# Sixteen batch ids in one register read instead of four

## The chip, the cores and the metric

The kernel runs on one core of a Trainium2 chip. The metric is the time of one execution on the device in microseconds (us); each kernel is run several times and the median is given. One execution is also profiled. The core has a matrix engine (PE, with the loading of its weights shown as PEld), a vector engine (DVE), a scalar engine (ACT), GpSimd (POOL) and SyncE (SP), which here issues the DMA transfers. Each engine runs its own list of instructions in order and waits on semaphores for the others. In the profile's rows an engine's name with a q (DVEq) is its instruction queue: register work and reads into registers, which are not counted as busy time of the engine.

## The reference

For each of 128 batches b, with an id `language_ids[b]` between 0 and 9 that selects the weights:

```python
w1 = W1[language_ids]
w2 = W2[language_ids]
h = jnp.einsum('bsh,bha->bsa', hidden_states, w1) + b1[language_ids][:, None, :]
h = jax.nn.relu(h)
adapted = jnp.einsum('bsa,bah->bsh', h, w2) + b2[language_ids][:, None, :]
x = hidden_states + adapted
...
return normed * gamma[language_ids][:, None, :] + beta[language_ids][:, None, :]
```

`normed` is `x` less its mean over the last axis, times `rsqrt(var + 1e-5)`, and the result is added to the input once more. x is (128, 128, 512) in float32; W1 is (10, 512, 128), W2 (10, 128, 512).

## The kernel before

One batch is one tile of 128 rows by 512. For each batch PE turns x by four transposes (`pxT`, line 440), ACT copies that to SBUF (`xT`, 444), PE multiplies by W1 (`down`, 463: four products, eight matmuls in the trace), ACT applies the bias and relu (`relu`, 471), PE multiplies by W2 (`up`, 477 or 485, into one of five PSUM tiles `py`), DVE adds the residual and its sum (`residual`, 503), ACT sums the squares (526), DVE scales by gamma (`scale`, 569) and finishes with rstd and the addend (`finish`, 578). POOL prepares two addends, x + b2 (450) and x + beta (457). SP loads x in pairs of batches and stores the outputs in pairs. For the first 17 batches SP fetches W1 of the batch's id from HBM (`load_first`, 276); later W1 of all ids lies in SBUF, and ACT or POOL copies the batch's part (`stage_w1`, 431), apart from some batches that SP loads (403, 692).

W2, b2, gamma and beta of all ten ids lie side by side in SBUF, and an instruction picks the batch's part by an address in a register of its own engine. So each of the five engines needs each id that it uses in its registers. The ids are loaded once into SBUF and clamped (`lang`, a row of 128 integers on one partition, line 253). `lid(b, engine)` (line 255) gives the register of batch b on an engine. When it is first asked for a batch of a group of four, it emits one instruction, `TENSOR_LOAD` (line 258), which reads the four ids of the group from `lang` into four registers; the other three batches of the group get theirs from the same read.

The order of the instructions is written out: the steps of all batches are put in a list `plan` with a due time counted in batches (`b` plus an offset from the table `STEPS`), sorted and emitted; the opening and the last batches are a plain list of calls. `keep` ties each instruction behind the one before on its engine. The reads have due times of their own: at `b + 0.99` ACT and PE ask for batch b + 5 and POOL for b + 6, so a read is emitted there when that batch begins a group. DVE's stand right behind `scale(b)` for each b that is a multiple of four, and read the group of b + 4. SP's come before the load that needs them.

Of the kernel before, what the change touches and what calls it, by code (L numbers as in the profile page):

```python
# [13 lines left out]
ET = mybir.EngineType  # L14
PSUM = bass.MemoryType.PSUM

P = 128
G = 4
X = 2
EPS = 1e-5  # L20
FIRST = 17
# [122 lines left out]
def cond_resid_kernel(ctx: ExitStack, tc: tile.TileContext, x, itok, W1, b1, W2, b2, gamma, beta, out):  # L144
# [11 lines left out]
    KC = H // P  # L156
    NG = B // G
    assert S == P and A == P and B % G == 0 and H % P == 0

# [3 lines left out]
    def keep(ins):  # L163

        engine = ins.ins.engine
        if engine in last:
            tc.add_manual_dep(ins.ins, last[engine], behind, reason="kept order")
        last[engine] = ins.ins.name
        return ins
# [16 lines left out]
    def load_x(g):  # L186
        t = xp.tile([P, X, H], FP, tag="x", name=f"x_{g}")
        keep(nc.sync.dma_start(out=t, in_=x[g * X : (g + 1) * X].rearrange("b s h -> s b h")))
        xs[g] = t

    def xb(b):
        return xs[b // X][:, b % X, :]

# [7 lines left out]
    def load_part(lo, hi, engine=nc.sync):  # L201
        xs[lo // X] = xp.tile([P, X, H], FP, tag="x", name=f"x_{lo // X}")
        keep(engine.dma_start(out=xs[lo // X], in_=x[lo:hi].rearrange("b s h -> s b h")))

# [41 lines left out]
    lids, w1s = {}, {}  # L246
# [4 lines left out]
    lang = const.tile([1, B], I32, name="lang")  # L251
# [1 line left out]
    keep(nc.vector.tensor_scalar(lang, lang, 0, L - 1, ALU.max, ALU.min))  # L253

    def lid(b, engine):
        g = b // G
        if (g, engine) not in lids:
            loads, vals = nc.values_load_multi_w_load_instructions(  # L258
                lang[0:1, g * G : (g + 1) * G],
                engines=[engine],  # L260
                min_val=0,
                max_val=L - 1,
                skip_runtime_bounds_check_because="clamped on the chip to 0..L-1 above",
            )
            for ins in loads:
                keep(ins)
            lids[g, engine] = vals
        return lids[g, engine][b % G]

# [1 line left out]
    def load_first(b):  # L273
        w1s[b] = wp.tile([P, KC, A], FP, tag="w1s", name=f"w1s_{b}")
        src = W1[bass.ds(lid(b, ET.SP), 1)].rearrange("o (p k) a -> p (o k a)", k=KC)
        keep(nc.sync.dma_start(out=w1s[b].rearrange("p k a -> p (k a)"), in_=src))  # L276
# [59 lines left out]
    def spread(r, copier):  # L336
        t = (beta_b, gamma_b, b2_b)[r // L]
        row = p_y.tile([P, H], FP, tag="y", name=f"row_{r}")
        pick_r = pick[:, r : r + 1].to_broadcast([96, P])
        keep(nc.tensor.matmul(row, lhsT=pick_r, rhs=parts[:96, :], start=True, stop=True))  # L340
        dst = t[:, r % L * H : (r % L + 1) * H]
        if copier is nc.scalar:
            keep(nc.scalar.copy(dst, row))  # L343
        else:
            keep(nc.vector.tensor_copy(dst, row))
# [9 lines left out]
    def shuffle_rows(lo, hi):  # L355
        for r in range(lo, hi):
            t = (beta_b, gamma_b, b2_b)[r // L]
            keep(nc.vector.stream_shuffle(t[:, r % L * H : (r % L + 1) * H], fours[0], [r] * 32))  # L358
# [8 lines left out]
    def of(parts, b):  # L367
        if b < len(parts[0]):
            return parts[0][b]
        return parts[1][b % steady] if b < closing else parts[2][b - closing]  # L370
# [16 lines left out]
    def b2_by_vector(b):  # L387
        return kind(b) == "D"
# [10 lines left out]
    def load_rows(b):  # L399
        w1s[b] = wp.tile([P, KC, A], FP, tag="w1s", name=f"w1s_{b}")  # L400
        rows = W1[bass.ds(lid(b, ET.SP), 1)].rearrange("o (i k r) a -> i (o r) k a", i=4, k=KC)
        for i in range(4):
            keep(nc.sync.dma_start(out=w1s[b][32 * i : 32 * (i + 1)], in_=rows[i]))
# [21 lines left out]
    def stage_w1(b):  # L425
        w1s[b] = wp.tile([P, KC, A], FP, tag="w1s", name=f"w1s_{b}")
        gpsimd = turn(b) == "c"
        v = lid(b, ET.Pool if gpsimd else ET.Activation)
        src = w1.rearrange("p l k a -> p (l k a)")[:, bass.ds(v * (KC * A), KC * A)]
        dst = w1s[b].rearrange("p k a -> p (k a)")  # L430
        keep(nc.gpsimd.tensor_copy(dst, src) if gpsimd else nc.scalar.copy(dst, src))  # L431
# [152 lines left out]
    def on(b):  # L584
        return 0 <= b < B
# [133 lines left out]
    x_turn(0)  # L719
    transpose_b1()  # L720
    spread(11, nc.scalar)
    for n in (0, G):
        lid(n, ET.PE)
    shuffle_rows(0, 10)
    x_turn(1)
    spread(12, nc.scalar)
# [31 lines left out]
    def at(when, step, *args):  # L758
        plan.append((when, len(plan), step, args))

    def when(name, b):
        return b + of(STEPS[name], b)

    for b in range(B):
        if b >= 20 and b % X == 0:
            at(b + X_STEPS[b // X - 10], load_x, b // X)
# [29 lines left out]
    def at_pair(g, key, step, *args):  # L796
        if g < E // 2 - 3 or (step, *args) in begun:
            at(key, step, *args)

    for g in range(E // 2 - 1):  # L800
        b = 2 * g
        for n in (b, b + 1):
            if b2_by_vector(n):
                at_pair(g, when("vb2", n), vector_b2, n)
            at_pair(g, when("stat", n), residual, n)
            at_pair(g, when("square", n), square, n)
        at_pair(g, when("means", b), scalar_means, g)
        at_pair(g, when("root", b), deviation, g)
        for n in (1, 2, 3):
            at_pair(g, when(f"n{n}", b), rstd, g, n)  # L810
        for n in (b, b + 1):
            at_pair(g, when("scale", n), scale, n)
            at_pair(g, when("end", n), finish, n)
        if b % G == 0 and on(b + G):
            at_pair(g, when("scale", b) + 0.001, lid, b + G, ET.DVE)
        at_pair(g, when("store", b), store, g)

    for _, _, step, args in sorted(plan, key=lambda step: step[:2]):
# [190 lines left out]
```

## Time and profile before

| | us |
|---|---|
| median of 3 runs | 300.58 |
| lowest and highest run | 299.26, 300.98 |
| the profiled execution | 300.62 |
| its span, first to last instruction | 298.9 |

TensorE's granted clock was 0.997 on average. The rows of the profile read: line, engine, operation, tile written <- tiles read, shape, count. In a timeline the first column is the start in us from the span's start, the second the duration of the group, and a bracket at the end gives the idle time of the engine before it and what ended it. The view of one line lists the number of its instructions and their shortest, median and longest duration in ns, with the first and last start.

### The profile page before, as it was taken

What the parts mean: (1) busy time and instruction counts of PE and PEld (TensorE: products, weight loads), DVE (VectorE), ACT (ScalarE), POOL (GpSimd) and SP (SyncE); (2) the same over time, 40 slices, a digit from 0 to 9 for tenths busy, and PEclk for the clock granted to TensorE, in tenths of its full rate; (3) what the DMA queues carried; (4) which work ended last, traced back from release to release, by engine and by line L of the source; (5) the groups of instructions that cost most, each with busy time, mean ns of one, the idle gap of its engine ahead of it and who ended that gap; (6) DMA issues with size and microseconds to landing.
All of it is one profiled execution on the core that took longest, in us unless ns stands there. A gap on an engine that the chain in (4) does not pass through costs nothing.

```text
span 298.9 us, 7366 instructions
## 1 busy us (share of the span) xinstructions
PE 290.5 (97%) x1783; PEld 215.7 (72%) x1783; DVE 288.5 (97%) x775; ACT 274.4 (92%) x761; POOL 276.8 (93%) x239
## 2 busy tenths in 40 slices
PE   7899999999999999999999999999999999999993
PEld 3658777777776777767777777777777777777760
DVE  6989999999999999899999999999999999999996
ACT  5878789999999999989999999999999999899993
POOL 1299998999999999999899999999899999999992
PEclk9999999999999999999999999999999999999998
DMA  6999999955978798986999399986989879884907
GB/s 226 392 388 368 345 330 401 404 221 182 325 242 315 232 315 208 374 278 211 326 303 356 134 302 289 335 276 217 333 220 397 288 258 281 314 274 147 313 4 281
DMA packets 61100, 85.22 MB, mean 285 GB/s; under 512 B 4057, under 2 KB 25060, under 8 KB 61058
## 3 DMA queue, kind: packets, MB, share of 16 engines
q1 hardware_dynamic: 60998, 84.71, 84.1%
q8 instruction: 15, 0.25, 0.3%
q14 instruction: 27, 0.22, 0.2%
q10 hardware_dynamic: 60, 0.05, 0.1%
HBM read 51.19 MB, written 33.55 MB: 284 GB/s over the span
## 4 chain that ended last, share of the span: by engine, by line
PE 75%; DMA 9%; POOL 6%; DVE 3%; issue 3%; SPq 1%; POOLq 1%; ACT 1%; ACTq 0%; DVEq 0%
PE ph L463 30%; PE py L485 23%; PE pxT L440 14%; PE py L477 8%; POOL o L457 3%; DMA out_dram<-o 3%; DMA w<-in_L_cond_W_dram 3%; POOL r L450 2%; DMA x<-in_x_dram 2%; DVE py L503 1%; DVE o L663 1%; SPq L276 1%; POOLq L258 1%; DVE n L669 0%; DVE py L569 0%
## 5 line engine op out<-in xcount | busy, mean ns | idle before, releaser
L457 POOL TENSOR_TENSOR o<-x,beta_b 128x512 f32<-128x512 f32 x121 | 153.8, 1297 | 14.4 <-DVE beta_b L358 11.6
L463 PEld LDWEIGHTS ph<-xT,w1s 128*128 128x128 f32 x1024 | 126.8, 192 | 14.8 <-ACT hT L471 8.5
L463 PE MATMUL ph<-xT,w1s 128*128 128x128 f32 x1024 | 135.5, 275 | 0.3 <-DMA w1s<-in_L_cond_W_dram 0.2
L450 POOL TENSOR_TENSOR r<-x,b_b 128x512 f32<-128x512 f32 x83 | 107.1, 1299 | 1.6 <-DMA x<-in_x_dram 1.6
L485 PE MATMUL py<-w,hT 128*128 x196 | 101.1, 598 | 0.2 <-DMA w<-in_L_cond_W_dram 0.2
L440 PEld LDWEIGHTS pxT<-ident,x 128*128 128x128 f32 x468 | 59.9, 150 | 53.4 <-issue 39.9
L569 DVE SCALAR_TENSOR_TENSOR py<-py,nmean,gamma_b 128x512 f32<-128x512 f32 x124 | 93.1, 752 | 0.0
L578 DVE SCALAR_TENSOR_TENSOR o<-py,rstd,o 128x512 f32<-128x512 f32 x116 | 85.7, 746 | 2.7 <-DVE py L569 1.6
L526 ACT ACTIVATE sq<-py,sum 128x512 f32<-128x512 f32 x124 | 85.5, 690 | 0.4 <-DVE rstd L545 0.3
L444 ACT COPY xT<-pxT 128x512 f32<-128x512 f32 x117 | 68.6, 586 | 5.6 <-PE pxT L440 5.5
L440 PE MATMUL pxT<-ident,x 128*128 128x128 f32 x468 | 71.2, 275 | 1.3 <-ACT gamma_b L343 0.7
L503 DVE SCALAR_TENSOR_TENSOR py<-py,r 128x512 f32<-128x512 f32 x88 | 60.8, 691 | 0.7 <-PE py L485 0.5
L471 ACT ACTIVATE hT<-ph,b1T 128x128 f32<-128x128 f32 x128 | 47.3, 369 | 8.2 <-PE ph L463 5.9
L431 ACT COPY w1s<-w 128x512 f32 x80 | 48.6, 618 | 1.2 <-issue 1.2
L485 PEld LDWEIGHTS py<-w,hT 128*128 128x128 f32 x196 | 29.9, 192 | 2.4 <-DMA w<-in_L_cond_W_dram 0.7
L477 PE MATMUL py<-w,hT 128*128 x60 | 30.7, 594 | 0.0
L526 ACT ACTIVATION_READ_ACCUMULATOR sq<-py,sum 128x1 f32 x124 | 25.5, 205 | 0.0
L503 DVE SCALAR_TENSOR_TENSOR py<-py,b_b 128x512 f32<-128x512 f32 x30 | 20.6, 688 | 0.0
L423 ACT COPY py<-x 128x512 f32<-128x512 f32 x30 | 17.9, 598 | 0.2 <-DVE o L578 0.2
L536 ACT ACTIVATE root<-ssq,eps 128x2 f32<-128x2 f32 x62 | 16.8, 271 | 0.4
L517 ACT ACTIVATE nmean<-sum 128x2 f32<-128x2 f32 x61 | 12.6, 207 | 0.5 <-DVE py L503 0.2
L503 DVE DVE_READ_ACCUMULATOR py<-py,r 128x1 f32 x88 | 12.3, 140 | 0.0
(80 smaller groups left out, 149.4 us busy)
## 6 DMA issues: line engine op xcount, KB each, us to landing
x<-in_x_dram SPq DMA_DIRECT2D x64, 512.0 KB, 5.6
out_dram<-o SPq DMA_DIRECT2D x62, 512.0 KB, 4.5
w1s<-in_L_cond_W_dram SPq DMA_DIRECT2D x25, 256.0 KB, 7.4
w1s<-in_L_cond_W_dram SPq DMA_DIRECT2D x44, 64.0 KB, 4.9
x<-in_x_dram SPq DMA_DIRECT2D x44, 64.0 KB, 2.3
w<-in_L_cond_W_dram SPq DMA_DIRECT2D x4, 640.0 KB, 8.1
w<-in_L_cond_W_dram SPq DMA_DIRECT2D x1, 1792.0 KB, 9.8
w<-in_L_cond_W_dram SPq DMA_DIRECT2D x1, 768.0 KB, 5.3
```

What stands on the lines that cost most here:

```text
L431: keep(nc.gpsimd.tensor_copy(dst, src) if gpsimd else nc.scalar.copy(dst, src))
L440: keep(nc.tensor.transpose(pxs[b][:, k, :], cols, ident))
L444: keep(nc.scalar.copy(xT[b], pxs.pop(b)))
L450: keep(nc.gpsimd.tensor_tensor(rs[b], xb(b), b2_b[:, bass.ds(v * H, H)], ALU.add))
L457: keep(nc.gpsimd.tensor_tensor(os[g][:, j, :], xb(b), beta_b[:, bass.ds(v * H, H)], ALU.add))
L463: nc.tensor.matmul(phs[b], lhsT=w1s[b][:, k, :], rhs=xT_of(b, k), start=(k == 0), stop=(k == KC - 1))
L477: keep(nc.tensor.matmul(ys[b], lhsT=hT[b], rhs=cols, start=False, stop=True, skip_group_check=True))
L485: keep(nc.tensor.matmul(ys[b], lhsT=hT[b], rhs=w2[:, bass.ds(v * H, H)], start=not m, stop=True))
L503: nc.vector.scalar_tensor_tensor(ys[b], ys[b], 1.0, r, ALU.mult, ALU.add, accum_out=sum_of(b))
L526: nc.scalar.activation(sq, ys[b], AF.Square, bias=col(sums, b), scale=-float(H), accum_out=col(ssqs, b))
L569: nc.vector.scalar_tensor_tensor(ys[b], ys[b], col(nmeans, b), gamma_b[:, bass.ds(v * H, H)], ALU.add, ALU.mult)
L578: nc.vector.scalar_tensor_tensor(o, ys[b], rstds[g][:, j : j + 1], o, ALU.mult, ALU.add)
```

## The change

A group is now sixteen batches for `lid`: one read brings sixteen ids into sixteen registers. `G = 4` remains for other uses. In the opening PE's two reads become one. In the pair loop DVE's read stands behind `scale(b)` for b a multiple of 16 and reads the group of b + 16. The reads of ACT, PE, POOL and SP follow from `lid` itself.

```diff
+IDS = 16
...
     def lid(b, engine):
-        g = b // G
+        g = b // IDS
         if (g, engine) not in lids:
             loads, vals = nc.values_load_multi_w_load_instructions(
-                lang[0:1, g * G : (g + 1) * G],
+                lang[0:1, g * IDS : (g + 1) * IDS],
...
-        return lids[g, engine][b % G]
+        return lids[g, engine][b % IDS]
...
-    for n in (0, G):
-        lid(n, ET.PE)
+    lid(0, ET.PE)
...
-        if b % G == 0 and on(b + G):
-            at_pair(g, when("scale", b) + 0.001, lid, b + G, ET.DVE)
+        if b % IDS == 0 and on(b + IDS):
+            at_pair(g, when("scale", b) + 0.001, lid, b + IDS, ET.DVE)
```

The lists of PE, DVE, ACT and POOL have 32 reads each before and 8 each with the change; SP's has 22 and then 8. No other instruction is added, removed or moved on any engine. Two places show it (all line numbers of the changed kernel are one higher).

DVE behind `scale(44)`, about 119 us into the span; `py` is the tile of a batch in PSUM, `o` the output. Before:

```order
L503 SCALAR_TENSOR_TENSOR py_2389,sum_2391<-py_2389,r_2308 128x512
L545 SCALAR_TENSOR_TENSOR rstd_2424<-part_2385,root_2384 128x2
L569 ISA
L569 SCALAR_TENSOR_TENSOR py_2226<-py_2226,nmean_2369,gamma_b 128x512
L258 TENSOR_LOAD lang
L578 SCALAR_TENSOR_TENSOR o_2194<-py_2288,rstd_2424,o_2194 128x512
```

With the change:

```order
L504 SCALAR_TENSOR_TENSOR py_2482,sum_2484<-py_2482,r_2419 128x512
L546 SCALAR_TENSOR_TENSOR rstd_2517<-part_2478,root_2477 128x2
L570 ISA
L570 SCALAR_TENSOR_TENSOR py_2331<-py_2331,nmean_2462,gamma_b 128x512
L579 SCALAR_TENSOR_TENSOR o_2299<-py_2399,rstd_2517,o_2299 128x512
```

The read of batches 48 to 51 is gone from this place; those ids come with the read behind `scale(32)`, where one stood before too, as DVE's list has it now:

```order
L570 ISA
L570 SCALAR_TENSOR_TENSOR py_1795<-py_1795,nmean_1891,gamma_b 128x512
L259 TENSOR_LOAD lang
L504 SCALAR_TENSOR_TENSOR py_1879,sum_1952<-py_1879,r_1863 128x512
L541 SCALAR_TENSOR_TENSOR part_1907<-ssq_1876,root_1906 128x2
```

That read is about 91 us into the span before; it keeps its place, and reads sixteen ids where it read four.

## Prediction

> **What bounds the kernel now.** I read the page first: busy shares, then the chain of waits.
>
> ```profile
> PE 290.5 (97%) x1783; PEld 215.7 (72%) x1783; DVE 288.5 (97%) x775; ACT 274.4 (92%) x761; POOL 276.8 (93%) x239
> PE 75%; DMA 9%; POOL 6%; DVE 3%; issue 3%; SPq 1%; POOLq 1%; ACT 1%; ACTq 0%; DVEq 0%
> ```
>
> PE is the bound, with DVE as busy as PE. A change can only gain what PE still loses between its matmuls, and DVE and ACT have little slack to take a delay. So the questions are what the reads of the ids (line 258) cost their engines, and how much of that reaches PE. The view of that line, all of the execution:
>
> ```profile
> L258 PEldq TENSOR_LOAD <-lang x32: 328/333/1140, 5.2 to 268.6; - x32
> L258 ACTq TENSOR_LOAD <-lang x32: 304/310/948, 8.0 to 268.6; - x32
> L258 DVEq TENSOR_LOAD <-lang x32: 340/344/1834, 18.5 to 273.7; - x32
> ```
>
> The columns are minimum/median/maximum in ns. A read of four ids is 0.31 to 0.34 us, whatever the engine, but some are far longer. Does one hold its engine up? The timeline of DVE around its two longest:
>
> ```profile
> L258 DVEq TENSOR_LOAD <-lang x1: 1834/1834/1834, 119.1 to 119.1; - x1
> 121.08 1.41 DVE L578 SCALAR_TENSOR_TENSOR o<-py,rstd,o 128x512 f32<-128x512 f32 x2 [0.84 <-DVE py L569]
> L258 DVEq TENSOR_LOAD <-lang x1: 1496/1496/1496, 223.2 to 223.2; - x1
> 224.80 1.41 DVE L578 SCALAR_TENSOR_TENSOR o<-py,rstd,o 128x512 f32<-128x512 f32 x2 [0.43 <-DVE py L569]
> ```
>
> L578 follows the read in the program, and both times it starts 0.1 to 0.2 us after the read has ended (119.1 + 1.83 = 120.9; 223.2 + 1.50 = 224.7). The bracket names L569, the instruction that ended last, yet what is waited for is the read. Thus a read is taken up ahead of the engine's own work and hides under it as long as it is shorter than its **room**, the time from its start to the start of the next instruction; beyond that the engine idles. ACT shows the same, and here the chain names the read:
>
> ```profile
> 132.57 0.52 ACTq L258
> 133.62 0.62 ACT L431 COPY w1s<-w 128x512 f32 x1 [0.53 <-issue]
> 168.04 0.62 ACT L431 COPY w1s<-w 128x512 f32 x1 [0.46 <-issue]
> ```
>
> **What the reads that go away cost PE.** The timeline of PE over these places:
>
> ```profile
> 125.96 0.60 PE L440 MATMUL pxT<-ident,x 128*128 128x128 f32 x4
> 126.56 1.12 PE L485 MATMUL py<-w,hT 128*128 x2
> 127.52 1.05 PE L463 MATMUL ph<-xT,w1s 128*128 128x128 f32 x8
> 128.55 1.13 PE L485 MATMUL py<-w,hT 128*128 x2
> ...
> 133.90 0.60 PE L440 MATMUL pxT<-ident,x 128*128 128x128 f32 x4
> 134.56 1.16 PE L463 MATMUL ph<-xT,w1s 128*128 128x128 f32 x8
> 135.55 1.02 PE L485 MATMUL py<-w,hT 128*128 x2
> ...
> 168.39 0.60 PE L440 MATMUL pxT<-ident,x 128*128 128x128 f32 x4
> 168.98 1.16 PE L463 MATMUL ph<-xT,w1s 128*128 128x128 f32 x8
> 169.97 1.02 PE L485 MATMUL py<-w,hT 128*128 x2
> ...
> 230.29 1.11 PE L485 MATMUL py<-w,hT 128*128 x2
> 231.24 1.05 PE L463 MATMUL ph<-xT,w1s 128*128 128x128 f32 x8
> 232.27 1.12 PE L485 MATMUL py<-w,hT 128*128 x2
> 233.23 0.60 PE L440 MATMUL pxT<-ident,x 128*128 128x128 f32 x4
> ```
>
> Undisturbed, a group starts 0.44 us after four pxT, 0.89 after eight ph, 0.86 after two py (rows 105.79 to 107.98 of the next fence). Here it is 0.60, 0.96, 1.03 after the long DVE read (0.40 too much), 0.66 and 0.99 after the ACT read of 132 (0.32), 0.59 and 0.99 after that of 167 (0.25), and 0.95, 1.03, 0.96 after the DVE read of 223 (0.33). Sum 1.30 us of PE for 0.84 + 0.53 + 0.46 + 0.43 = 2.26 us of idle engine, so **0.58 us of PE per us lost on DVE or ACT**.
>
> All four reads go: with sixteen ids the reads that stay are those where a batch of DVE's pair loop, or the batch that ACT and PE look ahead to, is a multiple of 16, and these four stand at others. Gain: **-1.3 us**. The other reads that go were hidden and give nothing.
>
> **What the reads that stay cost.** Eight stay on each engine, with 16 ids each. No row shows such a read. Bounds: 0.33 us, if it is one trip whatever it brings, and 4 x 0.33 = 1.32, if each id is a trip. The engines' minima (304, 328, 340) are too close together to tell. I take trips: a sequencer instruction without a read is short,
>
> ```profile
> L569 DVEq FUSED_REGOPS  x124: 57/57/57, 20.5 to 292.5; - x124
> ```
>
> so of DVE's 344 ns some 287 belong to four ids, 72 ns each, and sixteen make 57 + 16 x 72 = **1.2 us**, nearer to the high end. Now the rooms. PE, at one of the kept places:
>
> ```profile
> L258 PEldq TENSOR_LOAD <-lang x1: 331/331/331, 105.7 to 105.7; - x1
> 105.79 1.05 PE L463 MATMUL ph<-xT,w1s 128*128 128x128 f32 x8
> 106.68 0.60 PE L440 MATMUL pxT<-ident,x 128*128 128x128 f32 x4
> 107.12 1.02 PE L477 MATMUL py<-w,hT 128*128 x2
> 107.98 0.72 PE L463 MATMUL ph<-xT,w1s 128*128 128x128 f32 x5
> ```
>
> L477 is next after the read: room 1.42 us. A read of 1.2 and 0.1 to 0.3 to get going again nearly fills it: 0 to 0.14 lost at each of seven places, I take 0.07: **+0.5**. DVE, two kept places:
>
> ```profile
> L258 DVEq TENSOR_LOAD <-lang x1: 341/341/341, 90.7 to 90.7; - x1
> 91.44 0.69 DVE L503 SCALAR_TENSOR_TENSOR py<-py,r 128x512 f32<-128x512 f32 x1
> L258 DVEq TENSOR_LOAD <-lang x1: 346/346/346, 21.1 to 21.1; - x1
> 21.80 0.15 DVE L540 SCALAR_TENSOR_TENSOR part<-ssq,root 128x2 f32<-128x2 f32 x1
> ```
>
> Rooms 0.74 and 0.7, where 1.3 is wanted: 0.6 lost at each, 0.1 to 0.2 at two more (estimated), and some 0.4 at the first read, which only just precedes its user: 1.8 us. ACT has a room of 0.9 at a kept place, and there the read is long besides:
>
> ```profile
> L258 ACTq TENSOR_LOAD <-lang x1: 621/621/621, 244.6 to 244.6; - x1
> 245.49 0.37 ACT L471 ACTIVATE hT<-ph,b1T 128x128 f32<-128x128 f32 x1
> ```
>
> With one more such place and 0.1 here and there I put ACT at 1.2 us in all (an estimate). At 0.58, 3.0 us are **+1.7**. Long reads: kept places had them too, 621 ns on ACT above, and on PE and DVE
>
> ```profile
> L258 PEldq TENSOR_LOAD <-lang x1: 1060/1060/1060, 244.1 to 244.1; - x1
> L258 DVEq TENSOR_LOAD <-lang x1: 962/962/962, 56.3 to 56.3; - x1
> ```
>
> If their excess (0.73, 0.31, 0.62) comes once per read as now, PE loses about 0.6 and the others 0.93 x 0.58 = 0.5: **+1.1**. If it comes per id it is four times that, about +4.4.
>
> Taken at nothing: SP's first read holds back the first W1 loads by 0.9 us, with x and a part of W2 issued ahead of them for the DMA engines to work on; without that cover it costs 0.9. POOL's reads lie under its additions, some of them ahead. PE's two first reads become one, under the load of W2 that the first up waits for. Register work stays as it is.
>
> Sum: -1.3 + 0.5 + 1.7 + 1.1 = **+2.0 us** on the profiled execution's 300.62 (span 298.9 and 1.7 around it; the median of the runs is 300.58): **302.6 us**. Its own range: 301.0 (long reads and PE's share at nothing) to 304.3 (DVE and ACT losing twice the 3.0 us).
>
> [...]
>
> **The rivals.**
>
> *One trip whatever the count*: a read stays near 0.33 us and fits every room. Then only the gain is left, with some 0.3 (an estimate) for shorter delays behind other long reads that I did not count: 300.62 - 1.3 - 0.3 = **299.0**, faster. For it: four ids in 0.34, no more than six register instructions of 57 ns. Against it: nothing but the argument above. [...]
>
> *Trips, but covered*: a read takes 1.0 to 1.1, PE's rooms hold it, DVE and ACT make up their 2 to 3 us before it reaches PE's buffers (five py). Half of the +1.7 and nothing else: 300.62 - 1.3 + 0.9 = **300.2**, no change. For it: the read of 962 ns at 56.3 left no idle on DVE.
>
> *Long reads grow with the ids*: one of 1.06 becomes 4.2 and PE stands still for almost 3 us: 302.6 - 1.1 + 4.4 = **305.9**. It decides once an id's trip, not the read, meets the traffic. For it: every engine's maximum is three to five times its median, so what lengthens a read is no engine's own. Against it: no row tells whether a long read lost its time once or on each id.
>
> *Slow trips*: with sixteen, every trip is as slow as in the read of 962 ns, 0.24 us, so 3.9 a read; PE loses 3.9 + 0.1 - 1.42 = 2.6 at seven places, 18 us: 300.62 - 1.3 + 18 = **317**. Against it: 0.33 for four nearly always. [...]
>
> **How the numbers follow.** Chances: forecast 0.45, one trip 0.27, covered 0.15, growing 0.09, slow 0.04. About 0.5% (1.5 us) is what a measurement of this kernel can tell from no change. Slower: 0.40 of the forecast's, 0.01 of covered, 0.13 of the last two, together 0.54. Same: 0.05, 0.07 of one trip, 0.10 of covered: 0.22. Faster: 0.20 of one trip, 0.04 of covered: 0.24. The range 298.7 to 306.3 takes in all but the slow trip and some of the ends.
>
> **What would show it.** Line 258's row: 8 reads an engine, a minimum of 1.1 to 1.4 us is right, 0.35 is the first rival. The idle of 0.84, 0.53, 0.46 and 0.43 is gone. New idle after the read stands on DVE near 22 and 91 and on ACT near 245; py on PE after the kept reads is on time or 0.1 late. If the reads are 1.2 us and the time is still below 300.6, my factor of 0.58 is wrong; if PE waits for over 1 us at several reads, long ones grow.

## The result, and the profile after

| | before | the change |
|---|---|---|
| median | 300.7 | 304.87 |
| lowest and highest of 4 runs each | 299.26, 300.98 | 303.96, 305.48 |
| ratio to before, 95% interval | | 1.0146 [1.0104, 1.0187] |
| the profiled execution | 300.62 | 303.96 |
| its span | 298.9 | 302.2 |

The change makes the kernel slower by 1.5%, 4.2 us, where 2.0 were forecast. First the view of the line of the reads in the changed kernel, with shortest, median and longest duration in ns:

```profile
L259 SPq TENSOR_LOAD <-lang x8: 979/1028/3042, 3.1 to 245.6; - x8
L259 POOLq TENSOR_LOAD <-lang x8: 1049/1060/1894, 3.1 to 236.0; - x8
L259 PEldq TENSOR_LOAD <-lang x8: 1110/1122/1780, 5.2 to 247.1; - x8
L259 ACTq TENSOR_LOAD <-lang x8: 1009/1022/1222, 8.0 to 247.7; - x8
L259 DVEq TENSOR_LOAD <-lang x8: 1095/1210/2297, 20.7 to 232.3; - x8
```

There are eight reads an engine, and the shortest is 3.2 to 3.4 times as long as with four ids, not four times. Against the minima of before, twelve more ids cost PE 1110 - 328 = 782 ns and DVE 1095 - 340 = 755, 63 to 65 ns each; some 67 to 88 ns are left that do not depend on the count. The median is close to the minimum on four engines. On DVE it is not: several of its reads are long, and the longest takes twice the minimum. The timeline of DVE around three of them, each read with the instruction that follows it:

```profile
L259 DVEq TENSOR_LOAD <-lang x1: 1352/1352/1352, 20.7 to 20.7; - x1
22.33 0.70 DVE L496 TENSOR_TENSOR py<-py,b_b 128x512 f32<-128x512 f32 x1 [0.96 <-ACT sq L527]
L259 DVEq TENSOR_LOAD <-lang x1: 2297/2297/2297, 127.3 to 127.3; - x1
129.76 0.70 DVE L504 SCALAR_TENSOR_TENSOR py<-py,r 128x512 f32<-128x512 f32 x1 [1.41 <-PE py L486]
L259 DVEq TENSOR_LOAD <-lang x1: 1669/1669/1669, 162.8 to 162.8; - x1
164.66 0.70 DVE L504 SCALAR_TENSOR_TENSOR py<-py,r 128x512 f32<-128x512 f32 x1 [0.60 <-POOL o L458]
```

127.3 + 2.30 is 129.6, and DVE goes on at 129.76 after 1.41 us of idle time; 162.8 + 1.67 is 164.5, and it goes on at 164.66. The brackets name PE and POOL, but the read ends last, as it did behind the long reads of before. Of the 0.96 us in the opening only some 0.4 are new: the same instruction waited for PE there before,

```profile
19.79 0.70 DVE L495 TENSOR_TENSOR py<-py,b_b 128x512 f32<-128x512 f32 x1 [0.56 <-PE py L485]
```

which is counted with the other idle time of before in the table below. A fourth read, of 1.31 us at 232.3, leaves 0.46. A read of the shortest kind leaves nothing where its room is large enough:

```profile
L259 DVEq TENSOR_LOAD <-lang x1: 1095/1095/1095, 58.4 to 58.4; - x1
L259 DVEq TENSOR_LOAD <-lang x1: 1098/1098/1098, 92.6 to 92.6; - x1
```

PE, in the opening and behind its longest read, which starts at 247.1:

```profile
11.44 1.10 PE L441 MATMUL pxT<-ident,x 128*128 128x128 f32 x4 [1.91 <-DMA x<-in_x_dram]
12.76 1.82 PE L464 MATMUL ph<-xT,w1s 128*128 128x128 f32 x8
...
249.13 1.12 PE L478 MATMUL py<-w,hT 128*128 x2 [0.41 <-issue]
```

The 1780 ns read costs PE 0.41 us as the bracket has it; the seven others show nothing of the kind. The opening is new. PE waits 1.91 us for a pair of x, and the eight matmuls of the next `ph` take 1.82 us where 1.05 is usual. The windows view of PE (length, busy time, instructions, granted clock, DMA share, GB/s) says why, with before's row below:

```profile
10.90:14.30 3.40, 2.86 (x13) 0.51 1.03 392
```

```profile
10.90:14.30 3.40, 3.40 (x27) 1.00 1.05 394
```

The granted clock was 0.51 for 3.4 us. The first matmul of W2 (`up`, line 486) then starts at 18.40 in place of 16.16.

To see how much of this counts I split DVE's idle time, in every profile taken, into the gaps of over 0.1 us in which a read ends, at most 0.4 us before DVE goes on (called **read idle** from here on), and all the others between DVE's first and last instruction:

| kernel | read idle | other idle | span |
|---|---|---|---|
| before | 1.57 | 5.24 | 298.9 |
| the change | 3.44 | 6.51 | 302.2 |
| the change again (last experiment but one) | 5.41 | 5.01 | 302.9 |

DVE's own work is the same in all (288.5, 288.7 and 288.8 us). In the first profile of the change 1.9 us of the 3.3 are more read idle, and 1.3 are more of the other kind, in a late opening; in the second 3.8 of the 4.0 are read idle and the opening isn't late. Some 0.5 of the 1.9 and of the 3.8 is the wait for PE that counted as other idle before.

### The profile page after: what moved, and what is told of

It reads as the page before. It is cut to its first block, busy times and chain, and to the rows that moved or that the text cites. A ratio compares the mean times of both kernels' runs of the same rounds, so it can differ in the third digit from the quotient of the medians.

```text
span 302.2 us, 7266 instructions
## 1 busy us (share of the span) xinstructions
PE 291.5 (96%) x1783; PEld 216.8 (72%) x1783; DVE 288.7 (96%) x775; ACT 274.6 (91%) x761; POOL 276.9 (92%) x239
```

## The experiments

What had to be told apart: does the loss come from DVE's reads (that they hold DVE where they are), from SP's first read (which holds back the first loads), or from what PE, ACT and POOL pay? All kernels below make the number of ids a choice for each engine; each adds to this only what its own diff shows:

```diff
-IDS = 16
+IDS = {ET.SP: 4, ET.PE: 16, ET.Activation: 16, ET.DVE: 16, ET.Pool: 16}
...
-        g = b // IDS
+        n = IDS[engine]
+        g = b // n * n
...
-                lang[0:1, g * IDS : (g + 1) * IDS],
+                lang[0:1, g : g + n],
...
-        return lids[g, engine][b % IDS]
+        return lids[g, engine][b - g]
...
-        if b % IDS == 0 and on(b + IDS):
-            at_pair(g, when("scale", b) + 0.001, lid, b + IDS, ET.DVE)
+        n = IDS[ET.DVE]
+        if b % n == 0 and on(b + n):
+            at_pair(g, when("scale", b) + 0.001, lid, b + n, ET.DVE)
```

The line of the reads is 260 in them. Ratios are to before on the same chip, five rounds each, with the 95% interval in brackets.

**SP back to four ids, the rest sixteen.** This is the diff above as it stands.

> Sixteen ids on PE, DVE, ACT and POOL, four on SP. Theory A (the opening: SP's first read of sixteen ids, 1.18 us instead of 0.50, sends the first loads out 0.7 us later, and the x of batches 2 and 3 lands too late for PE's transposes): PE's wait for that x (1.91 us at 11.4 in the changed kernel) is gone, py starts at 16.2 us again and not at 18.4, the span falls by about 2.2 us from 302.2 to 300, the time to 302.6, ratio to before 1.004 to 1.009. Theory B (the delays behind the long reads on DVE, ACT and PE later on make up most of the loss): the span stays above 301.5 and the ratio at 1.012 or more.

1.0068 [1.0043, 1.0094], median 302.88: about half of the loss is gone. PE's wait for x in the opening is gone too. DVE's reads at the same places are still long: 1.11 us of idle time behind the one near 57, 1.03 near 126, 0.83 near 161. So SP has a part, and DVE another.

**SP alone with sixteen.**

```diff
+IDS = {ET.SP: 16, ET.PE: 4, ET.Activation: 4, ET.DVE: 4, ET.Pool: 4}
```

> Sixteen ids on SP alone, four on the others. Theory A: the opening loses its 2.2 us here too (py from 18.4 us on, PE waits near 11.4 for x), nothing else changes; time 302.4 to 303.2, ratio 1.006 to 1.010. Theory B: SP's reads lie ahead of the transfers by enough, time as before, ratio 0.998 to 1.003.

1.0011 [0.999, 1.0032]. The theory that put some 2 us on SP's first read falls at this size. Its opening is as late as the change's, in the timeline and the windows of PE:

```profile
11.24 1.10 PE L442 MATMUL pxT<-ident,x 128*128 128x128 f32 x4 [1.70 <-DMA x<-in_x_dram]
10.90:14.30 3.40, 3.06 (x14) 0.54 1.03 395
```

Its `up` starts at 18.41, 2.25 us behind before, and PE ends its work 1.15 behind: half of a late opening was won back here. In the median of twelve runs little of it is seen.

**DVE's reads in another place, all sixteen.** The read of the next sixteen batches stands behind `scale(4)`, `scale(20)` and so on, in place of `scale(0)`, `scale(16)`; nothing else differs from the change.

```diff
+IDS = {ET.SP: 16, ET.PE: 16, ET.Activation: 16, ET.DVE: 16, ET.Pool: 16}
...
+        if b % n == 4 and on(b - 4 + n):
+            at_pair(g, when("scale", b) + 0.001, lid, b - 4 + n, ET.DVE)
```

> The changed kernel, with DVE's reads four batches later: behind scale(b) for b = 4, 20, 36, ... instead of 0, 16, 32, ...; still sixteen ids, the same group. In the kernel before the reads of four ids at these places were 341 to 345 ns each time from b = 36 on, with rooms of 0.98 to 1.67 us. Theory C (a place decides, by its room and by whether reads there are lengthened): the reads are 1.10 us there, DVE's idle of 1.41, 0.60 and 0.46 us behind them falls to 0.2 us or less each, PE gains about 1.2 us; span 301.0, time 303.6, ratio 1.008 to 1.013. Rival D (sixteen ids meet the traffic wherever they are read): reads of 1.5 us and more remain at two or more of the places, and the time stays at 304.9, ratio 1.013 to 1.017.

0.9994 [0.9971, 1.0018]: the whole loss is gone, more than either theory gave, with the same number of reads, of the same size, on all engines. Two of DVE's reads at their new places, and the only long one of these:

```profile
L260 DVEq TENSOR_LOAD <-lang x1: 1101/1101/1101, 101.3 to 101.3; - x1
L260 DVEq TENSOR_LOAD <-lang x1: 1096/1096/1096, 135.5 to 135.5; - x1
L260 DVEq TENSOR_LOAD <-lang x1: 2240/2240/2240, 238.2 to 238.2; - x1
```

The read idle is 1.90, of which 0.95 stands behind the first read in the opening and 0.95 behind the last row. The opening was late here too (PE waits 1.58 us for x), by 1.38 us, and at the end none of that is left.

**Eight ids.**

```diff
+IDS = {ET.SP: 8, ET.PE: 8, ET.Activation: 8, ET.DVE: 8, ET.Pool: 8}
```

> Eight ids a read on all engines, 16 reads an engine. If the price is one trip for each id (four: 0.328 us on PE, sixteen: 1.110, so 65 ns an id and 67 fixed), the shortest read on PE is 0.59 us, on DVE 0.59, on SP 0.52. That fits every room; SP's first read then costs 0.2 us and the opening a part of its 2.2 (0 to 0.6). Time 299.8 to 301.4, ratio 0.997 to 1.003. If the price is by transfers of some other size, the shortest read is 0.33 us (as four) or 1.11 (as sixteen); in the latter case the ratio is above 1.010.

```profile
L260 PEldq TENSOR_LOAD <-lang x16: 587/670/1857, 5.1 to 261.8; - x16
L260 DVEq TENSOR_LOAD <-lang x16: 593/600/1696, 18.8 to 267.8; - x16
```

The price of a read was forecast right: 328, 587, 1110 ns on PE for 4, 8 and 16 ids, a straight line. The time was not: 1.0055 [1.0028, 1.0082] where 0.997 to 1.003 stood. A read of 0.6 us fits nearly every room, and yet DVE lost 0.85, 0.79 and 0.43 us behind three long reads (near 126, 161 and 268). PE lost 0.21 and 0.90 behind two long reads of its own; the second, of 1857 ns, starts at 261.8:

```profile
263.92 0.63 PE L442 MATMUL pxT<-ident,x 128*128 128x128 f32 x4 [0.90 <-PE ph L465]
```

So the kernel pays for reads that are long, rather than for their normal length, and here not on DVE alone: DVE's read idle is only 0.6 us more than before.

**DVE alone with sixteen, at the change's places.**

```diff
+IDS = {ET.SP: 4, ET.PE: 4, ET.Activation: 4, ET.DVE: 16, ET.Pool: 4}
```

> Sixteen ids on DVE alone, at the changed kernel's places; four on PE, ACT, POOL and SP. Theory C (DVE's reads at these places make the loss, since DVE has no slack to win back the time): idle of 0.8 to 1.5 us behind the reads near 126 and 161 us and of about 1 at the first read; ratio 1.004 to 1.008, as with SP alone at four (1.0068). Rival E (it takes the sixteen of PE and ACT too): ratio 0.999 to 1.003.

1.0057 [1.0028, 1.0085], with a read idle of 4.65. The longest read (2.69 us, against a minimum of 1.10) stands where the change has its longest one:

```profile
L260 DVEq TENSOR_LOAD <-lang x8: 1096/1224/2691, 18.7 to 231.9; - x8
129.37 0.70 DVE L505 SCALAR_TENSOR_TENSOR py<-py,r 128x512 f32<-128x512 f32 x1 [1.59 <-PE py L487]
```

**DVE alone with sixteen, at the other place.** The same, with `b % n == 4` as above.

> Sixteen ids on DVE alone, its reads behind scale(b) for b = 4, 20, 36, ...; four on the others. Theory C: no DVE read is lengthened but perhaps one, and the idle of 0.84, 0.30 and 0.43 us that the kernel before has behind its reads of b = 44, 76 and 92 is gone; PE gains 0.6 to 1.2 us, time 299.7 to 300.4, ratio 0.995 to 0.998. Rival F (the place helped only because other engines read sixteen too): ratio 0.999 or more.

0.996 [0.994, 0.998], median 299.63: faster than before. Between this kernel and the last one only the place of DVE's reads differs (of seven; the first is the same), and the time differs by 2.7 us in the medians. The page, DVE's reads, and DVE where the read of 134.1 is under way:

```profile
PE 290.4 (98%) x1783; PEld 216.5 (73%) x1783; DVE 287.8 (97%) x775; ACT 274.0 (92%) x761; POOL 276.6 (93%) x239
L260 DVEq TENSOR_LOAD <-lang x8: 1098/1102/1823, 18.7 to 236.6; - x8
L260 DVEq TENSOR_LOAD <-lang x1: 1098/1098/1098, 134.1 to 134.1; - x1
134.76 0.15 DVE L542 SCALAR_TENSOR_TENSOR part<-ssq,root 128x2 f32<-128x2 f32 x1
134.82 0.75 DVE L571 SCALAR_TENSOR_TENSOR py<-py,nmean,gamma_b 128x512 f32<-128x512 f32 x1
135.49 0.15 DVE L544 SCALAR_TENSOR_TENSOR part<-part,root 128x2 f32<-128x2 f32 x1
135.55 0.69 DVE L505 SCALAR_TENSOR_TENSOR py<-py,r 128x512 f32<-128x512 f32 x1
```

The read ends at 135.2 and DVE has no gap: what was queued ahead of it lasted longer. Read idle is 0.79 in all, 0.78 less than before, and the span is 297.0, 1.9 less.

**All sixteen at the other place, SP's first sixteen batches in fours.** The kernel of the third experiment, and

```diff
+        n = 4 if engine == ET.SP and b < 16 else IDS[engine]
```

> Sixteen ids on all engines with DVE's reads at b = 4, 20, 36, ..., and SP's ids of the first sixteen batches in four reads of four. Theory A (SP's first read of sixteen costs the opening 0.9 to 2.2 us that stay): PE no longer waits 1.6 us near 11 us for x, and the time falls by about 1.4 us under that of the same kernel with SP at sixteen (0.9994): ratio 0.993 to 0.997. Rival G (what PE loses in the opening is made up later, as long as DVE isn't held up, because DVE and PE are both close to full): ratio 0.997 to 1.001.

0.9975 [0.9959, 0.9991], just past the border between what the two theories gave, on the rival's side. Its profile has one read of DVE of 2759 ns (1.47 us idle). It does not tell whether SP's first read costs something: the intervals of this and the third experiment overlap.

**PE, ACT and POOL with sixteen, DVE and SP four.**

```diff
+IDS = {ET.SP: 4, ET.PE: 16, ET.Activation: 16, ET.DVE: 4, ET.Pool: 16}
```

> Sixteen ids on PE, ACT and POOL, four on DVE and SP. Theory C: their reads of 1.0 to 1.1 us nearly fit their rooms (PE 1.36 to 1.42, ACT 1.2 to 1.3), the idle of 0.53 and 0.46 us on ACT before w1s is gone, 0.1 to 0.5 at L471 comes in; ratio 0.997 to 1.002. Rival H (their reads cost as much as DVE's): ratio 1.004 or more.

1.0019 [0.9998, 1.0039]: as expected, next to nothing, though the reads are as long as in the change:

```profile
L260 PEldq TENSOR_LOAD <-lang x8: 1104/1122/1759, 5.1 to 245.1; - x8
L260 ACTq TENSOR_LOAD <-lang x8: 1007/1035/1317, 9.8 to 245.7; - x8
```

**DVE and SP with sixteen**, and **all but DVE with sixteen.**

```diff
+IDS = {ET.SP: 16, ET.PE: 4, ET.Activation: 4, ET.DVE: 16, ET.Pool: 4}
...
+IDS = {ET.SP: 16, ET.PE: 16, ET.Activation: 16, ET.DVE: 4, ET.Pool: 16}
```

> Sixteen ids on DVE and SP, DVE's reads at the changed kernel's places; four on PE, ACT and POOL. Alone they gave 1.0057 (DVE) and 1.0011 (SP). Theory J (what SP's first read costs the opening can be won back later only where DVE isn't held up by its reads): together more than their sum, ratio 1.009 to 1.014. Rival K (the parts add up): 1.005 to 1.008.

> Sixteen ids on PE, ACT, POOL and SP, four on DVE at the places of the kernel before. Theory C and J (DVE's reads are what makes the whole): ratio 1.000 to 1.005, although the opening is as late as in the change (py from 18.4 us or 17.5 on). Rival (the four engines without DVE hold most of the loss): 1.008 or more.

DVE and SP without the others give the whole loss, 1.0143 [1.0113, 1.0172]. All but DVE give 1.0007 [0.999, 1.0024]. So without DVE's reads there is no loss, and SP's only counts beside them: 0.11% for SP alone and 0.57% for DVE alone, 1.43% together, more than their sum. (These runs were on three chips, each beside before on its own; whether chips differ in this is open.) I had explained this by the late opening, won back only as long as DVE isn't held. The profile of DVE and SP doesn't bear that out: PE has no wait for x in its opening. What it has is more idle time behind DVE's reads, 1.15, 0.52, 1.08, 0.99 and 1.12 us behind five in a row from 56.9 on; four of these reads are over 2.1 us, and the one at 92.6 is of the shortest kind:

```profile
L260 DVEq TENSOR_LOAD <-lang x8: 1097/1744/2240, 19.1 to 233.0; - x8
59.17 0.16 DVE L542 SCALAR_TENSOR_TENSOR part<-ssq,root 128x2 f32<-128x2 f32 x1 [1.15 <-ACT sq L528]
129.28 0.70 DVE L505 SCALAR_TENSOR_TENSOR py<-py,r 128x512 f32<-128x512 f32 x1 [1.08 <-PE py L487]
200.01 0.70 DVE L505 SCALAR_TENSOR_TENSOR py<-py,r 128x512 f32<-128x512 f32 x1 [1.12 <-PE py L487]
```

Whether SP's reads move the transfers so that they meet DVE's more often was not tried by itself and stays open.

**The change again**, to see whether the same reads are long in another execution.

> The change itself once more, beside the two others on one chip: ratio 1.012 to 1.017 by all theories. Theory C: idle of DVE behind its reads near 92, 127, 162 and 232 us again, at least two of them over 0.4 us, since these places see reads lengthened more often than not. If the read times of the first profile were chance, the reads there are 1.10 us and the idle is under 0.2 us each.

1.0111 [1.0079, 1.0143]. At 127 and 163 they are long again, longer than at first, and one at 56.5 besides; the opening isn't late this time (PE waits 0.67 us for x, and its clock is 1.00):

```profile
59.05 0.16 DVE L541 SCALAR_TENSOR_TENSOR part<-ssq,root 128x2 f32<-128x2 f32 x1 [1.36 <-ACT sq L527]
129.66 0.70 DVE L504 SCALAR_TENSOR_TENSOR py<-py,r 128x512 f32<-128x512 f32 x1 [1.49 <-PE py L486]
165.31 0.70 DVE L504 SCALAR_TENSOR_TENSOR py<-py,r 128x512 f32<-128x512 f32 x1 [1.34 <-PE py L486]
```

**A version meant to be the best.** Only DVE has sixteen, at the places behind `scale(20)`, `scale(36)` and so on, and the first sixteen batches come in small reads, so that no long read holds the opening.

```diff
+DVE_READS = {0: 4, 4: 8, 8: 16, 20: 32, 36: 48, 52: 64, 68: 80, 84: 96, 104: 112}
...
+        if engine == ET.DVE and b < 16:
+            n = 8 if b >= 8 else 4
...
+        if b in DVE_READS:
+            at_pair(g, when("scale", b) + 0.001, lid, DVE_READS[b], ET.DVE)
```

> As the run with sixteen ids on DVE alone behind scale(b) for b = 4, 20, 36, ..., but the first ids in smaller reads (0 to 3, 4 to 7, then eight from 8) and the last read behind scale(104) and not scale(100), where it was lengthened in all three runs so far. Theory L (the span is the DVE's busy time plus its idle, whatever the other engines read): DVE's idle falls by the 0.4 to 0.6 us at the first read and the 0.37 at the last, to about 5 us in all, the span to 296.2 to 297.0, ratio 0.992 to 0.996. If PE or ACT bound it by now: span 297 or more and a ratio of 0.996 or more although DVE's idle falls.

```profile
L263 DVEq TENSOR_LOAD <-lang x10: 346/1100/1115, 18.7 to 248.1; - x10
```

Not one long read is left (read idle 0.19), and the ratio is 0.9968 [0.995, 0.9986], no better than the 0.996 of the simpler version: DVE waited 0.8 us more for other things (5.66 in place of 4.87), so its whole idle time did not fall, as both branches of the expectation had it. Why it waited more is open. Both beat before, by 0.3 to 0.4%.

**All profiles together.** DVE's read idle and the span of the fourteen profiles, one of each kernel, with the ratio, which is that of the medians:

| kernel | read idle | other idle | span | ratio |
|---|---|---|---|---|
| version meant to be the best | 0.19 | 5.66 | 297.5 | 0.9968 |
| DVE alone, other place | 0.79 | 4.87 | 297.0 | 0.996 |
| SP alone | 1.24 | 6.98 | 300.4 | 1.0011 |
| before | 1.57 | 5.24 | 298.9 | 1 |
| all but DVE | 1.87 | 6.63 | 300.7 | 1.0007 |
| all, DVE's at the other place | 1.90 | 5.43 | 298.8 | 0.9994 |
| PE, ACT, POOL | 1.99 | 6.07 | 300.2 | 1.0019 |
| eight ids | 2.19 | 6.20 | 300.2 | 1.0055 |
| the same place, SP's first in fours | 2.42 | 4.83 | 299.3 | 0.9975 |
| SP four | 3.16 | 5.51 | 301.0 | 1.0068 |
| the change | 3.44 | 6.51 | 302.2 | 1.0146 |
| DVE alone, the change's places | 4.65 | 4.96 | 301.3 | 1.0057 |
| the change again | 5.41 | 5.01 | 302.9 | 1.0111 |
| DVE and SP | 5.75 | 4.97 | 302.8 | 1.0143 |

That span goes with the sum of both columns says nothing, since DVE's work is nearly the same throughout (287.8 to 288.8 us). What tells is that the other idle time hardly shrinks where the read idle grows (by 0.15 us for 1 us, standard error 0.12): a straight line through the fourteen gives 0.94 us of span for 1 us of read idle (standard error 0.15, scatter 0.9 us about the line). What DVE loses behind a read is, within that, not made up.

## Why the prediction was right or wrong

**The price of a read: right in kind, a little high.** 1.2 us was forecast from a trip for each id, 1.0 to 1.1 is the shortest. The 57 ns of a register instruction and 72 for an id were near the 67 to 88 and 63 to 65 that three counts now give. The rival of one trip whatever the count falls with it, and so does that of slow trips.

**The room: right.** The idle time behind a read is what is left of the read beyond the work queued ahead of it, up to 1.59 us on DVE and 0.90 on PE; behind the first read DVE also waits for PE. The same read of 1.1 us costs nothing at 58.4, 92.6 or 134.1. But I took the room from the distance between the read's start and the next instruction in the profile of before, and that is no constant of the place: near 91 I saw 0.74 and forecast 0.6 us of loss; the change lost next to nothing there (the read starts at 92.6), as the read had more work ahead of it. In two other profiles (DVE and SP, and DVE alone) that read did leave 0.52.

**The gain of 1.3 us: the places right, the split not shown.** The idle times of 0.84 and 0.43 on DVE and 0.53 and 0.46 on ACT are gone in the change, and 0.30 at 190 on DVE that I had passed over. What ACT's two were worth stays open: over the fourteen profiles the price of ACT's read idle comes out as 0.66 with a standard error of 0.37, or as 0.32 with 0.47 if ratios are taken for spans.

**The term that was too small is the loss on DVE: "1.8 us" at short rooms plus a long read's excess of 0.62, at a factor of 0.58.** The total was forecast at 2.0 us and is 4.2. Both parts of this term were off.

*The idle time.* 2.4 us were forecast for DVE (1.8 + 0.62). The 0.4 at the first read came as forecast (0.96 less the 0.56 of before). Of the other 1.4 at short rooms, near 22, near 91 and at two more places, the first profile of the change shows nothing and the second 0.25. The long reads, put at 0.62, left 2.48 (1.41, 0.60 and 0.46) and 4.19 (1.36, 1.49 and 1.34). I had named one long read among DVE's kept ones, at 56.3; the same profile had two more:

```profile
L258 DVEq TENSOR_LOAD <-lang x1: 624/624/624, 125.5 to 125.5; - x1
L258 DVEq TENSOR_LOAD <-lang x1: 654/654/654, 229.2 to 229.2; - x1
```

These and the one at 56.3 are the places behind `scale(48)`, `scale(96)` and `scale(16)`. In the five profiles with sixteen ids at the change's places the read behind `scale(48)` was long each time (2.08 to 2.69 us), as was the one behind `scale(64)` (1.67 to 2.40), which was not long before; the one behind `scale(16)` was long in four, and the one behind `scale(32)` never. So one trace showed some of the places that matter, not all, and not how long the reads there become.

*The factor.* I compared what PE lost over a few groups with what DVE and ACT lost, and took the rest as absorbed. My reading now is that PE catches up over a few groups because five `py` lie between it and DVE, but that DVE, 95 to 97% busy, has little to catch up with. What is measured is 0.94 (standard error 0.15) for DVE's read idle at the end of the program, in place of 0.58. "PE is the bound, with DVE as busy as PE" put the accent on the wrong half of the sentence.

With the measured idle time, less the 0.56 that is not new, and the factor, (3.44 - 0.56 - 1.57) x 0.94 = 1.2 and (5.41 - 0.56 - 1.57) x 0.94 = 3.1 us; the spans grew by 3.3, with a late opening in the first profile, and by 4.0.

**What PE pays: forecast too high; ACT's idle time: about right.** PE's +0.5 for reads that nearly fill its room and the 0.6 for its long one stand against an idle time of 0.41 and 0.48 behind one read in the two profiles of the change. On ACT 1.5 us were put in place of the 0.99 of before, and 1.51 and 1.22 are there. PE, ACT and POOL together cost 1.0019 [0.9998, 1.0039], -0.1 to 1.2 us.

**Luck in the sum.** Sorted by engine, gains included, the forecast held 0.7 us for DVE, 1.4 for PE and ACT and nothing for SP. Alone they gave 1.7 [0.8, 2.6], 0.6 [-0.1, 1.2] with POOL, and 0.3 [-0.3, 1.0]; DVE and SP together gave 4.3 [3.4, 5.2]. What was missing is about 1 us on DVE itself and some 2 us that come only with SP's reads beside it. What PE was given too much made good a part of that, so the sum came nearer to the result than its parts.

**SP's first read, taken at nothing.** Alone it is nothing that can be measured, as forecast, though in some executions the cover fails: the read that starts at 3.1 takes 1179 ns in place of 500, the next loads are issued 0.7 us later, and PE waited 1.91, 1.70, 1.58, 0.67 or not at all. Together with DVE's reads SP's sixteen cost 0.9% (1.0143 against 1.0057), and that interplay was not in the prediction; its cause is open.

**Long reads that grow with the ids: no.** After the first 25 us, in the fourteen traces, on all engines but the two lists that mix sizes, the reads that are over 0.2 us longer than their engine's shortest are so by 0.94 us on the mean with sixteen ids (52 reads), 0.80 with eight (25) and 0.58 with four (199); in the change's trace alone 0.82 (9 reads) and in before's 0.60 (36). That is once per read and a little, not four times.

## What to carry to other kernels

In these runs a read of ids into registers cost its engine only what lay beyond the work queued ahead of it: nothing for the 1.10 us at 134.1 (DVE alone, other place), 1.59 us for the 2.69 us at 126.5 (DVE alone, the change's places). So on an engine that is busy to the end, as DVE is here at 95 to 97%, the question is where each read stands and how long it may become, not how many there are: eight large reads, seven of them moved to a better place, gained 0.4%; at the old places they lost 0.6%. Where the price grows with the ids as here, by 63 to 65 ns for each, larger reads save little, and they need larger rooms (1.10 us for sixteen ids on DVE, 0.34 for four). And a factor for "how much of this delay reaches the end" has to be taken at the end of the program, on the engine that is full, not from how soon its neighbour catches up.

## What the runs showed of the hardware

**Long reads go with traffic in packets of 2 KB.** Counted over the fourteen traces (1195 reads; the two lists that mix reads of different sizes are left out), none of 294 reads was over 0.2 us longer than its engine's shortest while fewer than 60 packets of 2 KB per us started; of 117 at 60 to 120 it was 17%, and of 784 at 120 or more 38%. In the traces of before and the change alone it was 0 of 47, 1 of 16 and 51 of 127. Each of these two traces has 35998 such packets; by the sizes of the arrays some 32800 of them, nine in ten, carry the x loads and the output stores (an estimate, with one packet for each row of 512 floats). This is a coincidence in time: no run took either away, so which of them lengthens the reads, and where they meet, is open. Place counts too: before's reads behind `scale(44)`, `scale(60)`, `scale(76)` and `scale(92)` were all long (1834, 732, 1359 and 1496 ns) and never those at four batches after a multiple of 16 (340 to 345 ns); that the transfers keep to a fixed place of the loop would fit this, but was not shown. But of these last the one behind `scale(100)` was long with sixteen ids in all three runs that had it (2240, 1823 and 2759 ns).

**The clock of PE fell to half after a wait of under 2 us.** In the change it was granted at 0.51 from 10.9 to 14.3 and in the run of SP alone at 0.54, after waits of 1.91 and 1.70 us; after one of 1.58, in the third experiment, it stayed at 1.00. The record of the granted clock in the change's trace reads 1.00 from 4.12 us on for 6.83 us, 0.50 from 10.94 for 3.41, 1.00 from 14.36 for 286.72, and then 0.50; before's reads 1.00 from 3.78 on for 293.55 us, and then 0.50. The four lengths are 2, 1, 84 and 86 times 3.41 us. The 3.41 us ahead of the fall, in the change and with SP alone, and for the third experiment a stretch of that length that holds most of the wait:

```profile
7.53:10.94 3.41, 1.73 (x11) 1.00 0.96 306
7.74:11.16 3.42, 1.52 (x10) 1.00 0.93 299
8.12:11.53 3.41, 1.83 (x13) 1.00 0.97 315
```

PE was busy for 1.73 and 1.52 us ahead of the two falls, and for 1.83 where the clock stayed. With the traces of before and the change divided into stretches of that length from 3.78 and 4.12 us on, PE worked 1.73 us in the stretch ahead of the fall in the opening, 0.05 and 0.00 in the two ahead of the falls at the end, and 2.47 or more in each of the others, none of which was followed by half the clock. What the clock goes by is not shown by so few falls; no run tried it by itself. The loss is 0.8 us for the `ph` shown, in two of fourteen profiles.
